# Dividing attention's output on chip, eight image rows at a time, and loading projection's input two groups ahead

## The chip, the cores and the metric

The kernel runs on one core of one Trainium2 chip. The metric is the device time of one execution in microseconds (us). The engines are named as in the profile: PE is the matrix engine (TensorE) and PEld its weight loads, DVE the vector engine, ACT the scalar engine, POOL the GpSimd engine, and SP the sync engine, which here issues every DMA. Each engine works through its own queue of instructions in order, and engines wait for one another through semaphores.

## The reference: two layers on a 48 x 48 image

The input is two images of 48 x 48 tokens with 768 channels. Two layers are applied one after the other, each added to its own input:

```
x = x + attention(groupnorm(x))     # 12 heads of 64, relative position terms, projection
x = x + spectral(groupnorm(x))      # 2-D FFT, two block-diagonal complex layers, inverse FFT
```

Only the first layer is touched by the change. Its attention, for each image and head, over S = 2304 tokens:

```
attn = (q * scale) @ k.T + rel_h[..., :, None] + rel_w[..., None, :]
attn = softmax(attn)
out  = attn @ v                     # 2304 x 64 per head
y    = out @ proj_w + proj_b        # 768 -> 768 over all heads
```

What matters here is where the softmax's division takes place. The kernel computes `exp(score - max)` without dividing, multiplies it with `v`, and scales the product by the inverse of the row's sum (the denominator) later, before projection.

## The kernel before, in words

**Stages.** For each of the two images in turn: `norm_transpose` normalises the image and lays it out with channels on partitions (`xnT`); `attention` runs all heads; `project_out` multiplies the heads' outputs with `proj_w` and adds the input; `Spectral` is the second layer. All matrix work is in 32-bit floats.

**Units of attention.** Heads are taken in six pairs (`pr`), so that two heads of 64 fill the 128 partitions. The 48 image rows are cut into six groups (`g`) of eight rows, 384 tokens; each group into three units (`x` = 0, 1, 2), 8 rows by 16 columns, 128 query tokens. The list `order` (L475) has the 108 units of an image. A unit is computed against all 2304 keys for both heads.

**What one unit needs.** `new_unit` (L340) adds the relative position terms `rhw` of rows and columns into a tile `s` of 128 x 2 x 2304: one POOL instruction a head (L344). There are four such tiles. `scores` (L354) lets PE make ten 128 x 512 pieces (the last two 128 x 256), and DVE adds each to `s` and keeps its maximum. The two heads alternate, so that DVE's second reduction is the first that needs the second head of `s`. `numerators` (L383) takes the exponential on ACT, with sums of the rows in `parts`. `squares` (L397) transposes 32 x 32 blocks on DVE, and `exchange` (L403) moves the blocks between partitions into `pT`, a quarter of them by ACT copies and the others by DMAs, six for each half of the unit. `weigh` (L417) multiplies with `v` on PE into the one bank of `ps_o`. `finish` (L434) copies that to a tile `res` of the group (ACT), reduces `parts` to a denominator (DVE, tile `dens`) and, after the group's last unit, stores `res` to the DRAM tensor `oT`.

**The order of the work.** It is written out by hand in the loop at L496. `InOrder` (L60) pins every instruction given through `pe`, `dve`, `act` and `sync` behind the one traced before it on that engine; the POOL instructions of `new_unit` are not pinned. Pass `n` runs the scores of unit `n`, the second half of the exchange of unit `n-1`, the first half of unit `n`, and the weighing of unit `n-2`; at its end `new_unit` prepares unit `n+1`. Beside the units, PE computes the queries of coming groups and the keys and values of the next head pair (`keys`, `values`, `queries`), one product a pass, so that the last pair has none of the keys and values left to make. `relative` (L289) makes the relative terms of a coming group in the pass with x = 0; they go to DRAM and come back skewed (`t<-rel`, `rhw<-t`). All matrix products but `ps_o` share seven PSUM banks in rotation (`ps_b`).

**The denominators before.** After three groups, `inverses` (L452) takes the reciprocals of 18 columns; a pass later PE transposes them (tile name `ps_i`), ACT copies them out, and three DMAs store them to the DRAM tensor `inv_d`.

**Projection before.** `Projection` (L576) lays its weights and token groups into the memory that `xnT` had. For a group of 384 tokens `parts` (L664) loads `oT` in two DMAs, loads the inverses spread over 64 partitions each in two more, and multiplies on POOL (128 x 2304). There are two buffers for tokens and one for inverses. The first steps (`late`, L533 and L560) run during the last passes of attention, and the products of the first tokens are filled in between the last units there. In `project_out` (L688) `tokens` is called one group ahead, from the loop over 18 tiles of 128 tokens, and POOL adds the bias to the rows of `x` (`rows`, L701).

Of the kernel before, what the change touches and what calls it, by code (L numbers as in the profile page):

```python
# [17 lines left out]
P = 128  # L18
HW = 48
S = HW * HW  # L20
C = 768
# [38 lines left out]
class InOrder:  # L60


    def __init__(self, tc, engine):
        self.tc, self.engine = tc, engine
# [95 lines left out]

def attention(tc, k, x_b, a, oT, inv_d, late, span, ps_b, ps_o):

# [11 lines left out]
    with ExitStack() as ctx:  # L176
# [14 lines left out]
        def bank(name):  # L191
            return ps_b.tile([P, 512], F32, tag="b", name=name)
# [12 lines left out]
        )  # L205
        bq = keep.tile([P, NP], F32, tag="bq", name="bq")
        bk = keep.tile([P, NP], F32, tag="bk", name="bk")
        rel = relp.tile([P, 2, 3, 2, RW], F32, tag="rel", name="rel")
        with ExitStack() as ctx2:
            small = ctx2.enter_context(tc.tile_pool(name="gn_s", bufs=1))  # L210
# [8 lines left out]
        pe, dve, act, sync = (  # L219
            InOrder(tc, e) for e in (nc.tensor, nc.vector, nc.scalar, nc.sync)  # L220
        )

        def project_T(w, parts):
# [116 lines left out]
        def new_unit(pr, g, x):  # L340
            qT, rhw = groups[pr, g]
            s = sp.tile([P, 2, S], F32, tag="s", name="s")
            for h in range(2):
                nc.gpsimd.tensor_tensor(  # L344
                    s[:, h, :].rearrange("p (y x) -> p y x", x=HW),
                    rhw[:, x, h, :HW][:, :, None].to_broadcast([P, HW, HW]),
                    rhw[:, x, h, HW:][:, None, :].to_broadcast([P, HW, HW]),
                    ALU.add,
                )
            return {"pr": pr, "g": g, "x": x, "qT": qT, "s": s}  # L350
# [78 lines left out]
                        skip_group_check=True,  # L429
                    )  # L430

        outs, dens = {}, {}

        def finish(un):  # L434

            pr, g, x = un["pr"], un["g"], un["x"]
            if x == 0:
                outs[pr, g] = outp.tile([P, 8, 3, 16], F32, tag="res", name="res")
                if g % 3 == 0:
                    dens[pr, g // 3] = outp.tile([P, 3, 2, 3], F32, tag="dens", name="dens")  # L440
            res = outs[pr, g]
            act.copy(res[:, :, x, :], un["o"][:, :P].rearrange("p (y d) -> p y d", d=16))
            dve.tensor_reduce(
                dens[pr, g // 3][:, x, :, g % 3], un["parts"], AX.X, ALU.add
            )
            if x == 2:
                sync.dma_start(
                    out=oT[pr * P : (pr + 1) * P, g * UQ : (g + 1) * UQ],
                    in_=res.rearrange("p y x d -> p (y x d)"),
                )  # L450

        def inverses(pr, half):  # L452


            den = dens.pop((pr, half)).rearrange("p x h g -> p (x h g)")
            inv = smallp.tile([P, 18], F32, tag="inv", name="inv", bufs=2)
            dve.reciprocal(inv, den)
            turned = outp.tile([18, P], F32, tag="turned", name="turned")

            def turn():  # L460
                tp = bank("ps_i")
                pe.transpose(tp[:18, :P], inv, k.ident)
                by_act.append(lambda: act.copy(turned, tp[:18, :P]))

            def send():
                dst = inv_d[pr, half].rearrange("h g (y x d) -> x (h g) y d", x=3, d=16)
                for x in range(3):
                    sync.dma_start(
                        out=dst[x],
                        in_=turned[6 * x : 6 * x + 6, :].rearrange("p (y d) -> p y d", d=16),  # L470
                    )

            return turn, send
# [18 lines left out]
        staged = ((0, 1), queries(0, 1))  # L492
        evict(by_act)
        recent = []
        last = turn = send = None
        for n in range(len(order) + 3):  # L496
            un = older = None
            if n < len(order):
                un = ahead
                pr, g, x = order[n]  # L500
                if g == 4 and x == 0 and pr + 1 < NP:
                    weights[0] = load_w(0, pr + 1)
                scores(un)
                recent.append(un)
            write = read = None
            if un is not None:
# [19 lines left out]
                if ready is not None:  # L526
                    key, qT = ready
                    rhw, write, read = relative(key[1], qT)
                    groups[key] = (qT, rhw)
            if turn is not None:  # L530
                turn()
                turn = None
            if n >= len(order) - 1 and recent:  # L533
                late(n - len(order) + 2)
            if n > 1 and recent:
# [3 lines left out]
            if last is not None:  # L539
                squares(last, 1)  # L540
                exchange(last, 1)
            if write is not None:
                write()
            if un is not None:
# [2 lines left out]
            evict(by_dve)  # L547
            if read is not None:
                read()
            if older is not None:  # L550
                finish(older)
            if un is not None and n + 1 < len(order):
                ahead = new_unit(*order[n + 1])
            if send is not None:
                send()
                send = None
            if older is not None and older["x"] == 2 and older["g"] % 3 == 2:
                turn, send = inverses(older["pr"], older["g"] // 3)
            if len(order) - 6 <= n <= len(order):
                late()  # L560
            last = un
# [14 lines left out]
class Projection:  # L576


    def __init__(self, tc, k, a, oT, inv_d, span, ps_b, dram):
# [3 lines left out]
        self.inv_d = inv_d  # L583
# [79 lines left out]

    def parts(self, g):  # L664

        at = [(NCC + 1) * C + i * NCC * UQ for i in range(3)]
        o_sb, inv = (
            self.whole[:, c0 : c0 + NCC * UQ].rearrange("p (cc s) -> p cc s", s=UQ)
            for c0 in (at[g % 2], at[2])
        )  # L670
        for h in range(2):
            cc = slice(h * NCC // 2, (h + 1) * NCC // 2)
            self.sync.dma_start(out=o_sb[:, cc], in_=self.oT_v[:, cc, g * UQ : (g + 1) * UQ])
            if h == 0:
                yield
        for h in range(2):
            self.sync.dma_start(
                out=inv[h * HD : (h + 1) * HD],
                in_=self.inv_d[:, g // 3, h, g % 3, :].partition_broadcast(HD),
            )  # L680
# [374 lines left out]
def block_kernel(tc, a, out):  # L1055
    nc = tc.nc
    B = a["x"].shape[0]
    with ExitStack() as ctx:
# [20 lines left out]
        for b in range(B):  # L1079
            oT = dram.tile([C, S], F32, tag=f"oT{b}", name=f"oT{b}")  # L1080
            y_d = dram.tile([YP, HW // 2, C], F32, tag=f"y_d{b}", name=f"y_d{b}")
            inv_d = dram.tile([NP, 2, 2, 3, UQ], F32, tag=f"inv_d{b}", name=f"inv_d{b}")
            ready = []

            def late(fill=0):
                if not ready:
                    ready.append(Projection(tc, k, a, oT, inv_d, span, ps_b, dram))
# [5 lines left out]
            attention(tc, k, a["x"][b], a, oT, inv_d, late, span, ps_b, ps_o)  # L1093
# [118 lines left out]
```

## Time and profile before

| what | value |
|---|---|
| runs without the profiler | median 3800.66 us of 3 (3797.74 to 3800.78) |
| the profiled execution: its time | 3804.1 us |
| its span, first to last instruction | 3802.2 us |
| mean granted clock of PE | 0.978 |
| attention of the first image, about | 70 to 1490 us |
| its projection, about | 1445 to 1640 us |
| DMA share of 16 engines, 120 to 1225 us | 0.76 |
| the same, 1225 to 1405 us (the last head pair) | 0.85 |
| POOL `s<-rhw`, 432 instructions | 1740.8 us, 4060 ns each |
| POOL idle before them | 1114.1 us |
| POOL multiply by the inverses in projection, 12 | 60.6 us |
| PE transposes of the inverses, 24 | 6.6 us |

How to read it: a row of the profile's groups names the line, the engine, the operation, what is written and read by the program's tile names, and the count; then busy time, the mean length of one, and how long the engine stood idle just before, with what ended the wait. The line of most attention instructions is L68, since `InOrder` issues them, so they are told apart by their tiles. In a timeline the first two numbers are start and length in us, "x4" is four instructions in a row, and the square bracket at the end is idle time of that engine before the row and what released it. SPq is SP's queue; its times are those of issuing a DMA, not of the transfer. In a row of windows the first numbers are the window and its length, then busy time and count for PE, PEld, DVE, ACT and POOL, then PE's granted clock, the DMA share and GB/s. A row of waits has who, for whom, the total, how many times, and the longest.

### The profile page before, as it was taken

To read this page: it belongs to the slowest core of one execution; us is meant where nothing else is said; L and a number is where in the kernel's file an instruction comes from. 1 tells how busy PE (TensorE), PEld (TensorE's weight loads), DVE (VectorE), ACT (ScalarE), POOL (GpSimd) and SP (SyncE) were. 2 spreads that over 40 slices of the span, in tenths; PEclk is the share of its full clock that TensorE was granted. 3 is DMA by queue.
4 is the path that set the end of the run, shared out by engine and by line. 5 is a ranking of instruction groups with operands and counts; after the bars stand their busy time and mean duration, and the time that the engine had idled before them with its cause. 6 is when DMAs were issued, how large, how long until landed. Compare 5 with 4: busy or idle time off the path is not lost.

```text
span 3802.2 us, 83341 instructions
## 1 busy us (share of the span) xinstructions
PE 3648.8 (96%) x31520; PEld 2592.3 (68%) x31520; DVE 2844.6 (75%) x6692; ACT 2519.5 (66%) x3692; POOL 1989.0 (52%) x598
## 2 busy tenths in 40 slices
PE   8999999999999888999989999999999999879999
PEld 6677776767777664566666767777677776645665
DVE  4788888888888983335557988889898898833445
ACT  3788888888888882133237888888888888821331
POOL 2565757575756663312125656566666666533121
PEclk9999999999999998999989999999999999889999
DMA  3677777777777887633526777777777778875334
GB/s 101 148 177 167 174 169 173 170 168 176 165 175 165 183 197 182 158 105 106 172 77 148 168 177 167 178 164 177 161 177 167 174 170 175 196 184 150 109 101 135
DMA packets 497822, 607.02 MB, mean 160 GB/s; under 512 B 180493, under 2 KB 312973, under 8 KB 497422
## 3 DMA queue, kind: packets, MB, share of 16 engines
q1 hardware_dynamic: 497422, 601.69, 67.6%
q8 instruction: 251, 4.11, 0.5%
q14 instruction: 149, 1.22, 0.1%
HBM read 131.61 MB, written 87.67 MB: 58 GB/s over the span
## 4 chain that ended last, share of the span: by engine, by line
PE 89%; DMA 4%; ACT 3%; DVE 2%; issue 1%; SPq 1%; POOL 1%; POOLq 0%; DVEq 0%; ACTq 0%
PE ps_o L68 23%; PE ps_s L68 21%; PE ps_proj L68 15%; PE ps_v L68 7%; PE acc L68 7%; PE ps L948 4%; PE ps_z L892 2%; PE ps L920 2%; PE ps_u L983 2%; PE ps L924 2%; PE ps_y L721 2%; PE ps_r L68 1%; ACT pT L68 1%; PE ps_x L1001 1%; DMA pT<-s 1%; DVE s L68 1%
## 5 line engine op out<-in xcount | busy, mean ns | idle before, releaser
L344 POOL TENSOR_TENSOR s<-rhw 128x2304 f32<-128x2304 f32 x432 | 1740.8, 4060 | 1114.1 <-DMA pT<-s 452.8
L68 DVE CUSTOM_DVE_ANT_0 s<-ps_s,s 128x512 f32<-128x512 f32 (+1 forms) x2160 | 1222.2, 633 | 359.4 <-issue 258.2
L68 ACT ACTIVATE s<-s,nm 128x1152 f32<-128x1152 f32 x864 | 1074.7, 1245 | 436.5 <-DVE nm L68 416.0
L68 DVE STREAM_TRANSPOSE s<-s 128x1152 f32<-128x1152 f32 x864 | 1111.8, 1344 | 5.5 <-ACT s L68 5.5
L68 ACT COPY pT<-s 32x1152 f32<-32x1152 f32 x864 | 993.3, 1150 | 21.5 <-PE ps_o L68 4.1
L68 PE MATMUL ps_o<-pT,v 128*64 128x128 f32 x15552 | 920.0, 278 | 49.7 <-ACT res L68 20.6
L68 PEld LDWEIGHTS ps_o<-pT,v 128*64 128x64 f32 x15552 | 868.2, 140 | 114.3 <-issue 50.7
L68 PE MATMUL ps_s<-kT,qT 64*128 64x512 f32 (+1 forms) x4320 | 908.8, 557 | 6.6 <-DVE mx L68 3.9
L68 PEld LDWEIGHTS ps_s<-kT,qT 64*128 64x128 f32 x4320 | 429.0, 186 | 436.6 <-issue 337.3
L68 PE MATMUL ps_proj<-xnT,w 128*128 128x384 f32 (+1 forms) x2016 | 596.4, 449 | 2.3 <-ACT gn_rstd L151 2.3
L68 PEld LDWEIGHTS ps_proj<-xnT,w 128*128 128x128 f32 x2016 | 360.0, 191 | 209.2 <-DVE mx L68 41.1
L68 PE MATMUL acc<-proj 128*128 128x384 f32 x864 | 288.7, 493 | 40.5 <-POOL proj L68 40.5
L742 DVE TENSOR_TENSOR x<-acc,x 32x384 f32<-32x384 f32 (+2 forms) x216 | 119.2, 553 | 276.8 <-PE acc L68 193.9
L68 PEld LDWEIGHTS ps_v<-w,xnT 128*128 128x128 f32 x2592 | 297.5, 194 | 21.2 <-DVE mx L68 21.2
L68 PE MATMUL ps_v<-w,xnT 128*128 128x128 f32 x2592 | 309.7, 279 | 0.0
L965 POOL TENSOR_TENSOR spectrum<-spectrum 128x480 f32<-128x480 f32 x80 | 96.3, 1204 | 342.0 <-DVE spectrum L964 195.8
L68 PEld LDWEIGHTS acc<-proj 128*128 128x128 f32 x864 | 166.1, 193 | 157.5 <-POOL proj L68 41.4
L728 ACT COPY y<-ps_y 112x384 f32<-112x384 f32 x96 | 46.0, 479 | 265.8 <-PE ps_y L721 264.5
L68 DVE DVE_READ_ACCUMULATOR2_ANT mx<- 128x1 f32 x2160 | 179.8, 83 | 0.0
L68 POOL TENSOR_TENSOR proj<-proj 128x2304 f32<-128x2304 f32 x12 | 60.6, 5049 | 222.4 <-DMA proj<-inv_d 185.3
L68 ACT ACTIVATION_READ_ACCUMULATOR s<-s,nm 128x1 f32 x864 | 161.1, 187 | 0.0
L928 ACT ACTIVATE spectrum<-ps,b 96x400 f32<-96x400 f32 x96 | 56.6, 590 | 146.5 <-PE ps L924 146.5
(98 smaller groups left out, 2096.5 us busy)
## 6 DMA issues: line engine op xcount, KB each, us to landing
pT<-s SPq DMA_DIRECT2D x2592, 144.0 KB
t<-rel SPq DMA_DIRECT2D x144, 189.0 KB
rhw<-t SPq DMA_DIRECT2D x144, 144.0 KB
y<-y_d SPq DMA_DIRECT2D x40, 360.0 KB
u_d<-spectrum SPq DMA_DIRECT2D x40, 360.0 KB
u<-u_d SPq DMA_DIRECT2D x48, 300.0 KB
xt<-in_x SPq DMA_DIRECT2D x12, 1152.0 KB
w<-in_qkv_w SPq DMA_DIRECT2D x36, 384.0 KB
```

The lines of the kernel that those rows point to most:

```text
L68: return lambda *args, **kw: self.tc.keep_in_program_order(op(*args, **kw))
L344: nc.gpsimd.tensor_tensor(s[:, h, :].rearrange("p (y x) -> p y x", x=HW), rhw[:, x, h, :HW][:, :, None].to_broadcast([P, HW, HW]), rhw[:, ...
L721: nc.tensor.matmul(ps[:YP, : 2 * SC], lhsT=k.fw, rhs=part[:, t0 : t0 + 2, ch], start=True, stop=True,)
L728: nc.scalar.copy(y1[:, :, ch], ps[:YP, : 2 * SC].rearrange("p (t c) -> p t c", c=SC))
L742: nc.vector.tensor_tensor(dst, acc[p : p + n, :UQ], dst, ALU.add)
L892: nc.tensor.matmul(ps[:BS, w * 96 : (w + 1) * 96], lhsT=self.y2[s, j][:, w, i * BS : (i + 1) * BS], rhs=k.fh, start=True, stop=True,)
L920: nc.tensor.matmul(ps[:BS, :400], lhsT=w1[:, wa, i, :], rhs=zf[:, 0, fs], start=True, stop=False,)
L924: nc.tensor.matmul(ps[:BS, :400], lhsT=w1[:, wb, i, :], rhs=zf[:, 1, fs], start=False, stop=True,)
L928: nc.scalar.activation(self.o1[:, ri, fs], ps[:BS, :400], AF.Gelu, bias=self.b1[:, n, ri : ri + 1])
L948: nc.tensor.matmul(ps[64 * r : 64 * r + 64, w * BS : (w + 1) * BS], lhsT=self.o1[:, ri, f0 : f0 + 64], rhs=w2[:, (0, 2, 1, 0)[2 * r + ri], ...
L965: nc.gpsimd.tensor_tensor(val, val, clip, ALU.subtract)
L983: nc.tensor.matmul(ps[: 2 * HW, :480], lhsT=k.ih, rhs=d2[:, c0 : c0 + 480], start=True, stop=True)
```

## The change

Attention now divides each group itself. In the pass after a group's last unit had its scores, `inverses` reduces the unit's sums, takes the reciprocal of a 128 x 32 tile `den` (six columns of it in use, all others one), transposes it in 32 x 32 blocks on DVE and stores it to a small DRAM tile. The function that it returns, `fetch`, is called a pass later, between the two halves of the exchange; it reads the inverses back in two DMAs, each spread over 64 partitions in runs of 96 numbers. When the group's last `res` copy is done, the next pass begins with `divide`, two POOL multiplies of 128 x 192; `store` sends `res` to `oT` in that pass, ahead of the first half of its exchange. The POOL instructions of `new_unit` are now pinned in program order too. The loop has one pass more. The PE transposes, their ACT copies and the three stores for every three groups are gone.

Projection loads `oT` alone, in two DMAs a group, into three buffers, and no longer multiplies. `tokens(2)` comes in the last step of attention, and from then on groups come two ahead, after the rows' loads.

```diff
-                nc.gpsimd.tensor_tensor(
+                pool_e.tensor_tensor(
                     s[:, h, :].rearrange("p (y x) -> p y x", x=HW),
...
+        def inverses(un):
+            key, x = (un["pr"], un["g"]), un["x"]
+            dve.tensor_reduce(
+                den[:, :6].rearrange("p (h x) -> p h x", x=3)[:, :, x], un["parts"], AX.X, ALU.add
+            )
+            if x < 2:
+                return None
+            turned = outp.tile([P, 32], F32, tag="turned", name="turned")
+            dve.reciprocal(turned, den)
+            dve.transpose(turned, turned)
+            inv_d = dp.tile([P * 32], F32, tag="inv_d", name="inv_d")
+            sync.dma_start(out=inv_d.rearrange("(p i) -> p i", i=32), in_=turned)
+
+            def fetch():
+                over[key] = inv = smallp.tile([P, 4, 3, 32], F32, tag="inv", name="inv", bufs=1)
+                for h in range(2):
+                    sync.dma_start(
+                        out=inv[h * HD : (h + 1) * HD].rearrange("p b x i -> p b (x i)"),
+                        in_=bass.AP(
+                            inv_d.tensor, inv_d.offset + 96 * h, [[0, HD], [1024, 4], [1, 96]]
+                        ),
+                    )
+            return fetch
+
+        def divide(key):
+            res = outs[key].rearrange("p (b y) x d -> p b y x d", y=2)
+            inv = over.pop(key).rearrange("p b x (y d) -> p b y x d", y=2)
+            for y in range(2):
+                pool_e.tensor_tensor(res[:, :, y], res[:, :, y], inv[:, :, y], ALU.mult)
...
-        for n in range(len(order) + 3):
+        for n in range(len(order) + 4):
             un = older = None
+            if whole is not None:
+                divide(whole)
...
-            if turn is not None:
-                turn()
-                turn = None
...
                 exchange(last, 1)
+            if whole is not None:
+                store(whole)
+                whole = None
+            if fetch is not None:
+                fetch()
+                fetch = None
             if write is not None:
                 write()
...
+            if last is not None:
+                fetch = inverses(last)
             if older is not None:
                 finish(older)
+                if older["x"] == 2:
+                    whole = older["pr"], older["g"]
...
-            if send is not None:
-                send()
-                send = None
-            if older is not None and older["x"] == 2 and older["g"] % 3 == 2:
-                turn, send = inverses(older["pr"], older["g"] // 3)
...
-            lambda: next(parts),
             lambda: list(parts),
             lambda: self.tokens(1),
+            lambda: self.tokens(2),
...
+        c0 = (NCC + 1) * C + g % 3 * NCC * UQ
+        self.o[g] = self.whole[:, c0 : c0 + NCC * UQ].rearrange("p (cc s) -> p cc s", s=UQ)
         for h in range(2):
             cc = slice(h * NCC // 2, (h + 1) * NCC // 2)
-            self.sync.dma_start(out=o_sb[:, cc], in_=self.oT_v[:, cc, g * UQ : (g + 1) * UQ])
-            if h == 0:
-                yield
-        for h in range(2):
-            self.sync.dma_start(
-                out=inv[h * HD : (h + 1) * HD],
-                in_=self.inv_d[:, g // 3, h, g % 3, :].partition_broadcast(HD),
-            )
-            if h == 0:
-                yield
-        self.pool.tensor_tensor(o_sb, o_sb, inv, ALU.mult)
-        self.o[g] = o_sb
-        yield
+            self.sync.dma_start(out=self.o[g][:, cc], in_=self.oT_v[:, cc, g * UQ : (g + 1) * UQ])
+            yield
...
         if t % 3 == 0 and 0 < t < NT - 3:
-            pr.tokens(t // 3 + 1)
             rows(t // 3 + 1)
+            if t < NT - 6:
+                pr.tokens(t // 3 + 2)
```

More of the change, by code (lines that the diff above doesn't have):

```diff
@@ L159, in norm_transpose, with attention @@
             )
-def attention(tc, k, x_b, a, oT, inv_d, late, span, ps_b, ps_o):
+def attention(tc, k, x_b, a, oT, late, span, ps_b, ps_o):
     nc = tc.nc
@@ L207, in attention @@
         bk = keep.tile([P, NP], F32, tag="bk", name="bk")
+        den = keep.tile([P, 32], F32, tag="den", name="den")
+        nc.gpsimd.memset(den, 1.0)
         rel = relp.tile([P, 2, 3, 2, RW], F32, tag="rel", name="rel")
@@ L218, in attention @@
         nc.vector.tensor_scalar(bk, bk, HD**-0.5, None, ALU.mult)
-        pe, dve, act, sync = (
-            InOrder(tc, e) for e in (nc.tensor, nc.vector, nc.scalar, nc.sync)
+        pe, dve, act, pool_e, sync = (
+            InOrder(tc, e) for e in (nc.tensor, nc.vector, nc.scalar, nc.gpsimd, nc.sync)
         )
@@ L430, in weigh @@
                     )
-        outs, dens = {}, {}
+        outs, over = {}, {}
+        def inverses(un):
[20 more added lines that the diff above has]
+            return fetch
@@ L434, in finish @@
         def finish(un):
-            pr, g, x = un["pr"], un["g"], un["x"]
+            key, x = (un["pr"], un["g"]), un["x"]
             if x == 0:
[L438 to L444, printed above, removed]
-            )
@@ L446, in finish @@
[L446 to L449, printed above, removed]
-                )
[L452 to L473, printed above, removed]
+                outs[key] = outp.tile([P, 8, 3, 16], F32, tag="res", name="res")
@@ new lines, in finish, with store @@
+            act.copy(outs[key][:, :, x, :], un["o"][:, :P].rearrange("p (y d) -> p y d", d=16))
+        def divide(key):
[3 more added lines that the diff above has]
+                pool_e.tensor_tensor(res[:, :, y], res[:, :, y], inv[:, :, y], ALU.mult)
+        def store(key):
+            pr, g = key
+            sync.dma_start(
+                out=oT[pr * P : (pr + 1) * P, g * UQ : (g + 1) * UQ],
+                in_=outs.pop(key).rearrange("p y x d -> p (y x d)"),
+            )
@@ L494, in attention @@
         recent = []
-        last = turn = send = None
-        for n in range(len(order) + 3):
+        whole = last = fetch = None
+        for n in range(len(order) + 4):
             un = older = None
+            if whole is not None:
+                divide(whole)
             if n < len(order):
@@ L576, with __init__ @@
 class Projection:
-    def __init__(self, tc, k, a, oT, inv_d, span, ps_b, dram):
+    def __init__(self, tc, k, a, oT, span, ps_b, dram):
         self.nc = nc = tc.nc
@@ L582, in __init__ @@
         self.oT_v = oT.rearrange("(cc p) s -> p cc s", p=P)
-        self.inv_d = inv_d
         self.whole = span.tile([P, NCC * S], F32, tag="span", name="proj")
@@ L664, in parts @@
     def parts(self, g):
[L666 to L670, printed above, removed]
+        c0 = (NCC + 1) * C + g % 3 * NCC * UQ
+        self.o[g] = self.whole[:, c0 : c0 + NCC * UQ].rearrange("p (cc s) -> p cc s", s=UQ)
         for h in range(2):
             cc = slice(h * NCC // 2, (h + 1) * NCC // 2)
-            self.sync.dma_start(out=o_sb[:, cc], in_=self.oT_v[:, cc, g * UQ : (g + 1) * UQ])
-            if h == 0:
-                yield
-        for h in range(2):
-            self.sync.dma_start(
-                out=inv[h * HD : (h + 1) * HD],
-                in_=self.inv_d[:, g // 3, h, g % 3, :].partition_broadcast(HD),
-            )
-            if h == 0:
-                yield
-        self.pool.tensor_tensor(o_sb, o_sb, inv, ALU.mult)
-        self.o[g] = o_sb
-        yield
+            self.sync.dma_start(out=self.o[g][:, cc], in_=self.oT_v[:, cc, g * UQ : (g + 1) * UQ])
+            yield
 def project_out(tc, k, x_b, pr, pools, y_d, x2, constants):
@@ L1081, in block_kernel @@
             y_d = dram.tile([YP, HW // 2, C], F32, tag=f"y_d{b}", name=f"y_d{b}")
-            inv_d = dram.tile([NP, 2, 2, 3, UQ], F32, tag=f"inv_d{b}", name=f"inv_d{b}")
             ready = []
@@ L1086, in late @@
                 if not ready:
-                    ready.append(Projection(tc, k, a, oT, inv_d, span, ps_b, dram))
+                    ready.append(Projection(tc, k, a, oT, span, ps_b, dram))
                 if fill:
@@ L1091, in late @@
                     ready[0].step()
-            attention(tc, k, a["x"][b], a, oT, inv_d, late, span, ps_b, ps_o)
+            attention(tc, k, a["x"][b], a, oT, late, span, ps_b, ps_o)
             with ExitStack() as ctx2:
```

## The prediction

> **What bounds the kernel now.** I read the page first, then who waited for whom on TensorE, then stages by window, then the timeline at the two places where the change acts.
>
> ```profile
> PE 3648.8 (96%) x31520; PEld 2592.3 (68%) x31520; DVE 2844.6 (75%) x6692; ACT 2519.5 (66%) x3692; POOL 1989.0 (52%) x598
> ```
>
> ```profile
> PE acc L68 <- POOL proj L68: 40.5, 2, 23.0
> ```
>
> ```profile
> 120.00:1225.00 1105.00, 1105.00 (x10317) 805.42 (x10315) 968.55 (x2304) 916.66 (x1261) 705.27 (x176) 1.00 0.76 170
> ```
>
> PE (TensorE) is the bound; its largest wait is for POOL (GpSimd) in projection, 40.5 us in two pieces, one an image. In the window that covers nearly all of head pairs 0 to 4 of the first image PE has no idle time at all (1105.00 of 1105.00). A PE delay there is paid in full.
>
> The two pieces, from PE's timeline at the end of attention:
>
> ```profile
> 1439.93 4.14 PE L68 MATMUL ps_pb<-proj,bv 128*128 128x384 f32 x12
> 1461.56 6.90 PE L68 MATMUL acc<-proj 128*128 128x384 f32 x12 [17.48 <-POOL proj L68]
> ...
> 3357.02 10.24 PE L68 MATMUL acc<-proj 128*128 128x384 f32 x24 [23.02 <-POOL proj L68]
> ```
>
> and what POOL waited for in the first:
>
> ```profile
> 1456.47 5.03 POOL L68 TENSOR_TENSOR proj<-proj 128x2304 f32<-128x2304 f32 x1 [37.99 <-DMA proj<-inv_d]
> ```
>
> The second half of the inverses is issued on SP at 1448.4, behind twelve pT transfers, lands at 1456.3, POOL multiplies until 1461.5, then PE starts.
>
> **Gains.** (1) The inverse loads and the 5 us multiply in front of the first product go. In the first image PE was free at 1444.1; the second oT half was issued at 1435.2. Next late is unit 106's pT, landed at 1448.4, just after the product. So the 17.5 us go, and 2.8 more because the product after the wait took 6.90 for 4.1 (clock 0.84 in this stretch). I keep 20. In the second image oT's last half was issued at 3330.7, just ahead of an inverse load landing at 3340.5; halving that queue puts oT near 3337, 3 us after PE is free: 23.0 + 2.1 - 3 = 22. (2) Twenty-four PE transposes go (row `ps_i` below, 273 ns of duration; in the chain of waits each takes 0.21): 5. Sum 47. Later projection groups already cost PE nothing: PE is busy 148.85 of 150 us in 1490 to 1640. The other removed work (12 POOL multiplies after the first, 24 ACT copies, 72 small stores) was beside PE and is worth nothing.
>
> **Costs.** Each group of eight rows now puts two small multiplies on POOL, in program order ahead of the bias sums `s` of a coming group. Today POOL runs ahead and needs only the rel-pos reads; afterwards it must also have the finished group's last `res` copy and the fetched inverses. One group in the steady stretch:
>
> ```profile
> 606.93 16.11 POOL L344 TENSOR_TENSOR s<-rhw 128x2304 f32<-128x2304 f32 x4 [12.12 <-DMA rhw<-t]
> ...
> 612.79 0.27 ACT L68 COPY res<-ps_o 128x128 f32<-128x128 f32 x1
> ...
> 601.82 1.26 SPq L68 DMA_DIRECT2D rhw<-t  x2
> 605.05 8.11 SPq L68 DMA_DIRECT2D pT<-s  x12
> ...
> 621.04 0.69 DVE L68 CUSTOM_DVE_ANT_0 s<-ps_s,s 128x512 f32<-128x512 f32 x1 [1.25 <-issue]
> ...
> 621.66 0.69 DVE L68 CUSTOM_DVE_ANT_0 s<-ps_s,s 128x512 f32<-128x512 f32 x1
> ```
>
> Read it so: POOL fills the x=0 unit of group G+2 from 606.93 to 615.0; DVE needs its second head at 621.66. The multiply for group G now stands before it. `res` of G's last unit is done at 613.06; with POOL's semaphore wait, 613.4. The fetch is issued after the sixth of the twelve pT issues (the seventh starts at 609.0). Its landing: the rhw reads take a median 5.5 us from first issue to POOL's start; the fetch has 512 packets for their 1,536, and 1,024 fewer at some 25 ns (the trace's mean for such packets) on 16 engines save 1.6: 3.9, so 612.8. `res` decides here; elsewhere, often the fetch. A multiply, from the groups by form (mean ns of one behind the busy time):
>
> ```profile
> L68 POOL TENSOR_TENSOR proj<-proj 128x2304 f32<-128x2304 f32 x12 | 60.6, 5049 | 222.4 <-DMA proj<-inv_d 185.3
> ...
> L68 POOL TENSOR_TENSOR x<-x,proj 96x768 f32<-96x768 f32 x48 | 85.2, 1808 | 1.2 <-PE ps_o L68 1.1
> ...
> L68 PE MATMUL ps_i<-ident,inv 128*18 128x128 f32 x24 | 6.6, 273 | 0.0
> ```
>
> The first two rows give 2.11 ns an element and 187 ns a call: 192 elements cost 0.59, two 1.2 (bounds 0.9 and 1.6, if short strided runs run faster or slower). Then 613.4 + 1.2 + 8.1 = 622.7: DVE's second head is 1.0 us late. Reading the same times for all groups with G+2 in pairs 0 to 4 (56, both images) gives late by 0.3 to 1.8, mean 1.0. PE feels it through the seven PSUM banks: the product after the scores needs the bank that DVE's fourth reduction frees (here 623.57), and today starts 0.28 us after that, at 623.85. Of this some 0.2 is slack, so PE stops 0.8: 56 x 0.8 = 45. PE cannot win it back, and SP, ACT and DVE behind it follow PE, so it repeats in every group. In the last pair PE has no next projections; pT packets end 3 us after issue instead of 1.5, so the fetch is later: late by 1.6 on average over 12 groups; DVE idles only some 14 us in 180 there (166.14 busy), so 1.4 each passes on: 17.
>
> DVE gets, per group, a wider reciprocal and a 128x32 transpose, some 0.4 us by the 128x18 reciprocal (0.27) and the 128x1152 transpose (1.34); in pairs 0 to 4 DVE waits 1.25 us or more before each unit's first reduction, so nothing; in the last pair 12 x 0.4, of which I count 2. Were that cover gone it would be 29 in all. The denominators' reduction only moves within its pass. SP gets three issues of 0.6 a group in place of one: store, write and fetch stand before pT transfers needed two passes later, and SP idles 2 us (603.1 to 605.05) and 3.5 us (613.8 to 617.3) before these pT batches, so nothing; without that slack the issues would be 72 x 1.2 us of SP time. The multiply's result is stored one pass later, long before its reader. Sum of costs: 45 + 17 + 2 = 64.
>
> **Two rules against the rows.** The Trainium skill, "DMA: Bandwidth & Descriptors", section "Anatomy of one DMA", puts a transfer (fitted on software-made descriptors) at about 2.0 us plus bytes over 436 GB/s. As an estimate the fetch would reach POOL about 3 us after its issue, `res` alone would decide, late would fall to some 0.75, costs to 45: no change. I take the rhw row's 3.9, measured behind the same pT queue. "GPSIMD Engine Reference", section "Engine selection", gives elementwise products to VectorE. There, two of 192 elements would take about 0.7 by the 384-element `x<-acc,x` row (0.55), inside DVE's idle time, POOL would never be late, and only the 47 gained would remain. The change takes POOL: its queue, not its speed, is what costs.
>
> **Rivals.**
> - *The lateness is absorbed* (faster): the multiply starts or runs 0.3 us sooner, or PE has more bank slack. From a mean lateness of about 0.8 down the 47 wins; at 0.4, costs are about 20: 3774. For it: half of the lateness is an extrapolated 1.2 us. Against: not one of the 68 groups reads on time. 22%.
> - *The fetch is held by its own write*: `inv_d`'s write goes out behind the rhw reads, about 603, and lands perhaps at 608; the fetch could go at 608.9. If the write takes 1 to 2 us longer, SP holds the fetch and the pT transfers behind it, and POOL is later by as much: 68 more per us, about 3890. For it: a margin of 1 us; against: SP waited for its `t<-rel` writes only four times, 5.3 us in all. 16%.
> - *The wait at the first product is not removed* but passes to oT's load or to the weights: the gain halves, 3840. 6%.
>
> **How the numbers follow.** 3804.1 for the profiled execution (span 3802.2 and 1.9 around it), minus 47, plus 64: 3821. The median of the runs is 3.4 lower: 3818. This case has 56% and its own range 3793 to 3850 (late by 0.75 to 1.4); within it 44% slower, 10% same, 2% faster. Within 0.2% (7.6 us) of before is what a measurement here can't tell from no change. With the rivals: faster 0.22, same 0.12, slower 0.66. The range 3778 to 3866 takes in most of the first rival and leaves out the worse half of the second.
>
> **What would show it.** Right: in the page POOL's idle time before `s<-rhw` is ended by ACT `res`, or by the inverse fetch through the multiply; DVE's reductions wait for POOL `s` in most groups, about 1 us each; PE idle before `ps_proj` or `ps_v` some 45 us, ended by DVE; `acc` waits for POOL gone; two multiplies of 0.6. Wrong: PE still at 1105 of 1105 in pairs 0 to 4, or multiplies far from 0.6, or SP waiting for DMA `inv_d<-turned`.

## The result, and the profile after

The changed kernel takes 3877.89 us (median of 4 runs, 3875.04 to 3890.09), the kernel before in the same series 3799.2 (4 runs, 3792.48 to 3800.78): ratio 1.0216 [1.0201, 1.0231]. Slower, as predicted, but by 79 us where 17 were forecast. The profiled execution took 3879.6 us, with a span of 3877.8 against 3802.2: 75.6 to explain.

Engine totals (the page) and the window that before was 1105.00 of 1105.00 for PE:

```profile
PE 3720.3 (96%) x31496; PEld 2605.6 (67%) x31496; DVE 2885.5 (74%) x6812; ACT 2515.7 (65%) x3668; POOL 2006.8 (52%) x732
```

```profile
120.00:1225.00 1105.00, 1089.37 (x9879) 775.38 (x9876) 948.29 (x2268) 880.69 (x1205) 699.41 (x223) 1.00 0.75 169
```

PE now has holes in this window, and 9879 products fall into it where 10317 did. The waits:

```profile
POOL res L68 <- DMA inv<-inv_d: 990.3, 69, 26.4
...
DVE s L68 <- POOL s L68: 169.6, 84, 22.8
...
PE ps_s L68 <- DVE mx L68: 61.0, 59, 2.8
```

and, in the kernel before, DVE's row for POOL's bias sums:

```profile
DVE s L68 <- POOL s L344: 54.6, 21, 23.0
```

PE's row for POOL in projection is gone. In its place POOL waits for the fetched inverses ahead of 69 of its 72 pairs of multiplies, DVE for POOL's bias sums 84 times (21 before), PE for DVE 59 times. PE's timeline at both images' first projection products shows the gain that was hoped for (the first row is the work in front of the first image's; the last two rows are the second image's):

```profile
1498.76 4.14 PE L68 MATMUL ps_pb<-proj,bv 128*128 128x384 f32 x12
1502.73 4.03 PE L68 MATMUL acc<-proj 128*128 128x384 f32 x12
...
3434.47 2.20 PE L68 MATMUL acc<-proj 128*128 128x384 f32 x6
3438.82 6.07 PE L68 MATMUL acc<-proj 128*128 128x384 f32 x18 [2.15 <-DMA proj<-oT]
```

In the first image no wait is left. In the second one of 2.15 us is left after six products, and the oT load ends it.

To place the 75.6 us I cut both executions at the same instructions: DVE's `nm` reductions (each follows the last piece of a unit's scores) of units 6, 90 and 107, the last `res` copy, and the last product of projection. The two images stand before and after the plus sign; the last column is the prediction's sum.

| stretch | before | after | moved | predicted |
|---|---|---|---|---|
| pairs 0 to 4 (unit 6 to 90) | 1056.1 + 1056.0 | 1099.4 + 1106.5 | +93.9 | +40 (45, less 5 for PE transposes) |
| last pair (unit 90 to 107) | 204.5 + 208.1 | 217.8 + 217.1 | +22.2 | +19 (17 and 2) |
| unit 107 to the last `res` | 53.9 + 55.3 | 33.6 + 33.0 | -42.6 | -42 |
| last `res` to the end of projection | 153.5 + 149.7 | 153.5 + 149.6 | 0 | 0 |
| everything else | | | +2 | 0 |

One term is wrong: pairs 0 to 4. One group there, somewhat later than most, in the order POOL, SP, ACT, DVE, PE (each from that engine's timeline):

```profile
634.28 1.14 POOL L68 TENSOR_TENSOR res<-res,inv 128x192 f32<-128x192 f32 x2 [15.96 <-DMA inv<-inv_d]
635.38 24.15 POOL L68 TENSOR_TENSOR s<-rhw 128x2304 f32<-128x2304 f32 x6
...
629.12 1.30 SPq L68 DMA_DIRECT2D inv<-inv_d  x2
...
632.40 0.27 ACT L68 COPY res<-ps_o 128x128 f32<-128x128 f32 x1
...
643.49 0.69 DVE L68 CUSTOM_DVE_ANT_0 s<-ps_s,s 128x512 f32<-128x512 f32 x1 [2.13 <-POOL s L68]
...
639.41 3.70 PE L68 MATMUL ps_s<-kT,qT 64*128 64x512 f32 x16
644.25 1.31 PE L68 MATMUL ps_s<-kT,qT 64*128 64x256 f32 x4 [1.13 <-DVE mx L68]
```

`res` is ready at 632.67. The fetch is issued at 629.12, but POOL's multiplies start only at 634.28, 5.16 us after it. They end at 635.4; two bias sums of 4.06 follow, up to 643.46, and at 643.49 DVE makes the reduction that had waited 2.13. PE then stands 1.13 us as the row shows, and its four small products take 1.31 where a twenty-product batch without a wait takes 4.14 in all, which is 0.46 for these four by their columns: 0.85 more of waiting lies inside the row. PE loses 1.98 (1.13 and 0.85) of DVE's 2.13.

Over the 56 groups whose delay falls into the first row of the table, the time from the fetch's issue to the multiply has a mean of 4.88 us (3.9 was taken), the multiply begins 1.47 after `res`, the pair of multiplies takes 1.14 (1.2 was taken), and DVE waits 1.65 (1.0 was taken for late).

### The profile page after: what moved, and what is told of

Its sections match the earlier page's. It is cut to its first block, busy times and chain, and to the rows that moved or that the text cites. A ratio compares the mean times of both kernels' runs of the same rounds, so it can differ in the third digit from the quotient of the medians.

```text
span 3877.8 us, 83832 instructions
## 1 busy us (share of the span) xinstructions
PE 3720.3 (96%) x31496; PEld 2605.6 (67%) x31496; DVE 2885.5 (74%) x6812; ACT 2515.7 (65%) x3668; POOL 2006.8 (52%) x732
## 3 DMA queue, kind: packets, MB, share of 16 engines
q14 instruction: 153, 1.25, 0.1%
## 4 chain that ended last, share of the span: by engine, by line
PE 50%; DVE 17%; POOL 13%; DMA 8%; SPq 8%; issue 3%; ACT 1%; POOLq 0%; DVEq 0%; ACTq 0%
DVE s L68 15%; POOL s L68 13%; PE ps_o L68 10%; SPq L68 8%; PE acc L68 7%; PE ps_s L68 7%; PE ps_v L68 6%; DMA pT<-s 6%; PE ps_proj L68 5%; PE ps L946 4%; PE ps L918 2%; PE ps_u L981 2%; PE ps_z L890 2%; PE ps L922 2%; PE ps_y L718 1%
## 5 line engine op out<-in xcount | busy, mean ns | idle before, releaser
L68 PE MATMUL ps_s<-kT,qT 64*128 64x512 f32 (+1 forms) x4320 | 972.6, 562 | 64.2 <-DVE mx L68 61.0
L68 POOL TENSOR_TENSOR res<-res,inv 128x192 f32<-128x192 f32 x144 | 82.5, 594 | 1069.0 <-DMA inv<-inv_d 990.3
L926 ACT ACTIVATE spectrum<-ps,b 96x400 f32<-96x400 f32 x96 | 56.6, 590 | 145.8 <-PE ps L922 145.8
```

What stands on the lines that cost most here:

```text
L68: return lambda *args, **kw: self.tc.keep_in_program_order(op(*args, **kw))
L926: nc.scalar.activation(self.o1[:, ri, fs], ps[:BS, :400], AF.Gelu, bias=self.b1[:, n, ri : ri + 1])
```

## The experiments

The theory from the two traces: the gain is as predicted, and the loss is POOL's lateness, of which the fetch's landing, not `res` and not the multiplies, is the greater part. Rival: something else in the change slows pairs 0 to 4 (the multiplies themselves, the pinning, the extra SP issues, the write).

**The multiplies behind the bias sums.** POOL's order alone is changed; the store of `res` goes out a pass later.

```diff
-            if whole is not None:
-                divide(whole)
...
             if un is not None and n + 1 < len(order):
                 ahead = new_unit(*order[n + 1])
+            if whole is not None:
+                divide(whole)
+                done, whole = whole, None
```

> The change with one move: the two multiplies of a finished group stand behind, not ahead of, the bias sums of the next group's first unit on POOL (and the store one pass later). Theory (place in POOL's queue): in pairs 0 to 4 the 94 us lost there go, in the last pair most of the 22, while the 43 won at the first product and the transposes' 5 stay: 3755 us, 3745 to 3770; DVE hardly ever waits for POOL's sums. Rival (the added DMA issues and small packets delay the pT transfers, or DVE's extra work): the multiplies' place is indifferent, 3850 to 3880.

3762.38 us, ratio to before 0.9905 [0.9887, 0.9923]. Pairs 0 to 4 take 1056.4 + 1055.0, what they took before. The multiply's row in the groups:

```profile
L68 POOL TENSOR_TENSOR res<-res,inv 128x192 f32<-128x192 f32 x144 | 82.9, 597 | 107.7 <-ACT res L68 64.2 <-DMA inv<-inv_d 43.5
```

As many multiplies, equally long, and 43.5 us of waiting for the fetch in place of 990.3. The same work with the same SP issues costs nothing once the sums that DVE waits for stand ahead of it. That rules out the multiplies, the pinning, the SP issues and the write as costs of their own in pairs 0 to 4.

**No wait for the inverses.** The multiplies stay in front but take a constant tile of ones; the fetch is still issued. Attention's output stays undivided here.

```diff
-                pool_e.tensor_tensor(res[:, :, y], res[:, :, y], inv[:, :, y], ALU.mult)
+                pool_e.tensor_tensor(
+                    res[:, :, y],
+                    res[:, :, y],
+                    one[:, None, :, :].to_broadcast([P, 4, 3, 16]),
+                    ALU.mult,
+                )
```

> The change with its multiplies taken by a constant one in place of the fetched inverses, which are still computed, stored and fetched, but not used: the output is left undivided. The multiplies keep their place in POOL's queue and wait for the res copy alone. In the changed kernel the multiply starts 1.5 us after res on average in pairs 0 to 4 and 2.1 in the last pair. Theory: those 1.5 go from a loss of 1.8 a group, 56 x 1.5 = 84 and about 19 in the last pair: 3775 us, 3760 to 3800. If the multiplies' own length and the res copy set the delay: 3850 or more. Rival (DMA or DVE load): 3878.

3780.80 us, ratio 0.9952 [0.9937, 0.9967].

```profile
L68 POOL TENSOR_TENSOR res<-res,ones 128x192 f32<-128x192 f32 x144 | 82.3, 592 | 970.1 <-ACT res L68 864.8 <-issue 69.0 <-DMA inv<-inv_d 25.1
```

The multiply now starts 0.08 us after `res`, DVE waits 0.28 on average, pairs 0 to 4 take 1061.1 + 1060.8. So `res` and two multiplies in front of the sums cost some 10 us in pairs 0 to 4; the wait for the fetch costs the other 84 of the 94, the clock (below) included.

**The same bytes in long runs.** The inverses are written so that the 384 of a head lie together: the two fetches have 128 packets of 1,536 bytes in place of 512 of 384. The tile's layout follows; the multiplies still take 592 ns.

```diff
-            sync.dma_start(out=inv_d.rearrange("(p i) -> p i", i=32), in_=turned)
+            sync.dma_start(
+                out=bass.AP(inv_d.tensor, inv_d.offset, [[32, 4], [128, 32], [1, 32]]),
+                in_=turned,
+            )
...
-                            inv_d.tensor, inv_d.offset + 96 * h, [[0, HD], [1024, 4], [1, 96]]
+                            inv_d.tensor, inv_d.offset + 384 * h, [[0, HD], [1, 384]]
```

> The change with the inverses laid out in DRAM so that a head's 384 are contiguous: the fetch reads one run of 1536 bytes for each partition in place of four of 384 (128 packets for 512); the write has as many runs as before. In the changed kernel the fetch's packets span 2.6 us, from 1.4 to 4.0 after its issue, though 512 packets of 22 ns on 16 engines fill only 0.7. If the number of runs makes that span, the last packet comes at about 2.8, the landing 1.2 us sooner, 56 x 1.2 and some 14 in the last pair: 3797 us, 3785 to 3815. If it is a fixed latency of a read through two issues: 3870 to 3880.

3808.54 us (13 runs), ratio 1.0021 [1.0012, 1.003].

```profile
L68 POOL TENSOR_TENSOR res<-res,inv 128x192 f32<-128x192 f32 x144 | 82.3, 592 | 994.5 <-DMA inv<-inv_d 582.6 <-ACT res L68 373.2 <-DMA pT<-s 25.1
```

From issue to multiply it is now 3.8 us on average, close to the 3.9 that the prediction took. `res` and the fetch share the releases, as the prediction had read from the trace of before. DVE waits 0.68, pairs 0 to 4 take 30.3 more than before and the last pair 14. With about the landing that was assumed, the kernel's time is within 10 us of the 3818 that was predicted, so this run isolates the term that failed. It is below 3818 because another term was too high (POOL's start after `res`, next section): pairs 0 to 4 lose 30 where 40 were predicted.

**The fetch sooner.** It is issued ahead of the second half of the exchange, six pT transfers earlier.

```diff
             evict(by_act)
+            if fetch is not None:
+                fetch()
+                fetch = None
             if last is not None:
                 squares(last, 1)
                 exchange(last, 1)
...
-            if fetch is not None:
-                fetch()
-                fetch = None
             if write is not None:
                 write()
```

> The change with the fetch issued one batch of six pT transfers earlier in the same pass. It would be issued some 4.4 us sooner, about 3.8 us after its own write was issued. Theory: res becomes the last thing that the multiply waits for, as with no wait for inverses: 3775 us, up to 3800 as the pT issues come 1.3 us later. Rival (the write's landing holds the fetch, and SP with it): SP waits for inv_d<-turned in every group, the fetch gains only part of the 4.4, 3800 to 3870.

3861.41 us, ratio 1.0159 [1.0133, 1.0186]: the rival's range, not the theory's. SP's waits for the inverses' write, here and (second row) in the changed kernel as it is:

```profile
SPq L68 <- DMA inv_d<-turned: 223.6, 72, 4.6
...
SPq L68 <- DMA inv_d<-turned: 5.3, 6, 2.9
```

PE's waits for pT, here and (second row) before:

```profile
PE ps_o L68 <- DMA pT<-s: 86.3, 53, 7.0
...
PE ps_o L68 <- DMA pT<-s: 18.9, 8, 4.6
```

POOL is hardly late here: DVE's second reduction, the one that waited 1.65 us after the change, waits 0.04 on average. But SP, in order, stands in each of the 72 groups for the inverses' write to land, 3.1 us on average (223.6 / 72), and the pT transfers queued behind go out late. In pairs 0 to 4, which take 61.8 us more than before, PE now waits 56.6 us ahead of `ps_o` products (0.2 before). The wait did not go, it changed its queue.

**The multiplies on DVE**, with the order of the first experiment.

```diff
-                pool_e.tensor_tensor(res[:, :, y], res[:, :, y], inv[:, :, y], ALU.mult)
+                dve.tensor_tensor(res[:, :, y], res[:, :, y], inv[:, :, y], ALU.mult)
```

> The change with the multiplies on DVE instead of POOL, at the end of the same pass, when the inverses have long landed. Theory (place in POOL's queue): POOL is never late, DVE takes about 0.7 us a group into its waits of 1.25 us before each unit; only the last pair, where DVE has little idle time, may give back 12 x 0.7 = 8: 3765 us, 3755 to 3775, like the kernel with the sums first. Rival (DVE has no room): 36 groups x 2 x 0.7 = 50 more, 3810.

4006.08 us, ratio 1.055 [1.0527, 1.0573]: far outside both. The operation's own record (min, median and max in ns), then one pair on DVE's timeline and the sums on POOL's:

```profile
L68 DVE TENSOR_TENSOR res<-res,inv x144: 342/1854/4209, 166.9 to 3586.1; 128x192 f32<-128x192 f32 x144
```

```profile
575.12 4.40 DVE L68 TENSOR_TENSOR res<-res,inv 128x192 f32<-128x192 f32 x2
...
566.94 12.09 POOL L68 TENSOR_TENSOR s<-rhw 128x2304 f32<-128x2304 f32 x3
```

The first multiply starts just after POOL began the third sum (about 575.0) and ends about 0.2 us after that sum does, at 579.03 (566.94 + 12.09); the second, with POOL idle, takes 0.35. So throughout: 38 multiplies that met no POOL instruction take 0.346, at most 0.36; the 106 that met one take a median 2.84, up to 4.21, and 105 of them end 0.2 to 0.3 us after that sum. Pairs 0 to 4 grow by 200 us, of which some 69 are PE's clock (see the run with a second multiply).

**Projection's groups one ahead**, the change otherwise whole (one late step fewer goes with it).

```diff
-            lambda: self.tokens(2),
...
-            if t < NT - 6:
-                pr.tokens(t // 3 + 2)
+            pr.tokens(t // 3 + 1)
```

> The change with projection's groups coming one ahead, as before. Theory: the gain at the first product is that of the loads and the multiply taken away, and a group's load has a whole group's products (some 25 us) to land: 3878 us, no difference from the changed kernel (within 8). Rival (two ahead is what removes the wait): PE waits for proj<-oT before the second or third group, 5 to 10 us an image, 3890 to 3900.

3889.21 us, ratio 1.0234 [1.0213, 1.0255]. That is 11 us above the change, just more than the 8 allowed for, but the interval overlaps the change's. The stretches at the end of attention and in projection agree with the change's (68.6 against 66.6 us, and 303 in both). So the rival's waits in projection aren't there; whether two ahead is worth a few us elsewhere can't be told from these runs.

**Before, with POOL's sums pinned in program order** (`pool_e` in place of `nc.gpsimd` in `new_unit`).

> The kernel before with POOL's bias sums pinned in program order, and nothing else. Theory: they run in this order anyway and no multiply stands ahead of them: 3799 us, no difference. Rival (the pinning itself makes POOL late): a part of the 94 us lost in pairs 0 to 4 shows up, 3820 or more.

3801.1 us (12 runs), ratio 1.0004 [0.9993, 1.0014]: pinning costs nothing that these runs can show.

**Before, without the inverses in projection.** Neither their loads nor the multiply remain there; the division is left out.

```diff
-            self.sync.dma_start(
-                out=inv[h * HD : (h + 1) * HD],
-                in_=self.inv_d[:, g // 3, h, g % 3, :].partition_broadcast(HD),
-            )
...
-        self.pool.tensor_tensor(o_sb, o_sb, inv, ALU.mult)
```

> The kernel before, whose projection neither loads the inverses nor multiplies by them: the division is left out, though the inverses are still made and stored, and tokens still come one ahead. Theory: this is the whole gain at the end of attention, 42 us, and nothing else changes: 3757 us, 3750 to 3765; PE's wait for POOL's proj gone. Rival (the wait passes to the next late thing, oT or pT): less than half of it, 3780 or more.

3757.35 us, ratio 0.9893 [0.9875, 0.9911]. The end of attention takes 33.6 + 34.7 us, as after the change: nearly all of the -42.6 by itself.

**A second multiply.** After each multiply by the inverses comes one by ones, which leaves the values as they are: about 1.2 us more on POOL for each group.

```diff
                 pool_e.tensor_tensor(res[:, :, y], res[:, :, y], inv[:, :, y], ALU.mult)
+                pool_e.tensor_tensor(
+                    res[:, :, y],
+                    res[:, :, y],
+                    one[:, None, :, :].to_broadcast([P, 4, 3, 16]),
+                    ALU.mult,
+                )
```

> The change with each of its two multiplies followed by a second one of the same size by a constant one on POOL, ahead of the bias sums. Theory (every delay at this place in POOL's queue is paid by PE, without slack): 2 x 0.57 = 1.14 us more for each of 56 groups in pairs 0 to 4 and about as much for 12 in the last pair, 78 us more than 3878: 3955 us, 3940 to 3965. Rival (part of the delay is absorbed downstream): 3900 to 3930.

4056.09 us, ratio 1.0673 [1.0655, 1.069]: 178 more than the change, where 78 were expected. (The profiled execution was the fastest of the five, 147.5 us above the change's; what follows is read from it.) The multiplies are no longer than before (595 ns), so the price of a late us was about twice what was expected. In the first image's group at 615 us, PE's timeline, and then windows of 1 us there (PE busy, PE's granted clock, DMA share, GB/s):

```profile
620.71 3.70 PE L68 MATMUL ps_s<-kT,qT 64*128 64x512 f32 x16
626.89 1.83 PE L68 MATMUL ps_s<-kT,qT 64*128 64x256 f32 x4 [2.48 <-DVE mx L68]
628.65 6.95 PE L68 MATMUL ps_proj<-xnT,w 128*128 128x384 f32 x12
```

```profile
625.00:626.00 1.00, 0.00 (x0) 1.00 0.91 233
626.00:627.00 1.00, 0.11 (x1) 1.00 0.99 230
627.00:628.00 1.00, 1.00 (x3) 0.76 0.93 226
628.00:629.00 1.00, 1.00 (x3) 0.50 0.37 81
...
633.00:634.00 1.00, 1.00 (x3) 0.50 0.00 0
634.00:635.00 1.00, 1.00 (x4) 0.83 0.00 0
```

After a hole of 2.48 us the granted clock falls to 0.50 for 7 us, and twelve products that take 4.14 elsewhere take 6.95. Adding up one minus the clock over pairs 0 to 4 gives the time lost to it: 0 before, 9.1 us after the change, 70.4 here. Of the 126.5 us by which pairs 0 to 4 grew against the change, 61.3 are the clock; the other 65.2 are 1.16 for each of 56 groups. That is about the POOL time added, and about what DVE's second reduction waits longer (2.82 against 1.65). So the term that this run was to measure is confirmed at about 1 to 1 in pairs 0 to 4, and a second one came with it. (The sum takes PE as busy while its clock is low, as it is in the window shown.) The last pair grew by 15.7 us, but by 15.1 in the same sum of the clock: the 14 expected there from the multiplies' own time aren't seen, and why is open.

**Sums first, long runs, and the fetch behind the first half of the next exchange**: what the runs pointed to.

```diff
             if un is not None and n + 1 < len(order):
                 ahead = new_unit(*order[n + 1])
+            if whole is not None:
+                divide(whole)
+                done, whole = whole, None
...
                 exchange(un, 0)
+            if fetch is not None:
+                fetch()
+                fetch = None
```

> The kernel with the sums first, its inverses in long runs, and the fetch issued behind the second batch of pT transfers of its pass instead of ahead of it. The multiply there has some 2 us to spare after the landing, and long runs land 1.2 us sooner. Theory (the fetch has slack now, pT transfers should not stand behind it): no worse than 3762 us, at best the 3757 of the kernel without any inverses in projection; 3755 to 3764. Rival (the multiply becomes late again, now for the sums of the group's second unit, which have about 2 us to spare): 3775 or more.

3756.54 us, ratio 0.9882 [0.9867, 0.9897], the fastest version; its interval overlaps that of sums-first alone (0.9905), so the two further steps aren't shown to gain. In the window of pairs 0 to 4 PE is whole again:

```profile
120.00:1225.00 1105.00, 1105.00 (x10309) 804.79 (x10306) 984.37 (x2357) 917.12 (x1254) 735.73 (x234) 1.00 0.78 175
```

## Why the prediction was right in sign and wrong in size

- **Gain at projection's first product, -42.** Right: -20.3 and -22.3. The oT load is late next in the second image, as said, by 2.15 us after six products.
- **PE transposes, -5.** Too high: in the fastest version, where PE has no hole in the window shown, pairs 0 to 4 take 2.1 less than before.
- **The failed step: the fetch's landing, "the fetch has 512 packets for their 1,536 ... 3.9".** It took the rhw reads' 5.5 us and took off packets at their mean time spread over 16 engines. Measured from issue to multiply: 4.88 in pairs 0 to 4, 5.01 in the last pair. The first packet comes 1.4 us after the issue and the last ends at 4.0 (medians), though 512 packets at their mean 25 ns over 16 engines fill only 0.8. So a mean packet time over 16 engines does not give a landing; with 128 packets for the same bytes the last ends at 3.0. "`res` decides here; elsewhere, often the fetch" turned with it: the fetch decided in 69 of 72 groups, and late was 1.65 by DVE's wait, not 1.0. The rest of that sum holds: read from the trace of before for the same groups, it gives 0.99 with 3.9 and 1.84 with 4.88.
- **A term of that sum that was too high**, and hid a part of the error: "with POOL's semaphore wait, 613.4". POOL starts 0.08 after `res` when it waits for that alone, not 0.34 as there, and late is then 0.28, where the prediction had 0.75.
- **"Of this some 0.2 is slack".** About right, if anything too much: (93.9 + 2.1 - 9.1) / 56 = 1.55 of 1.65 reaches PE; 1.98 of 2.13 in the group shown.
- **A term missing among the costs: PE's clock.** 9.1 us in pairs 0 to 4. In the last pair the same sum is 34.2, against 27.3 before: up to 6.9 of its 22.2. That is an upper bound, since PE is not always busy there, and it differs between executions (39.3 in the run with projection's groups one ahead).
- **The last pair, +19.** Near at +22.2, but partly by chance: DVE's second reduction waits 2.5 us there, not the 1.6 taken for late, so less of it passed on than the prediction held, and a part of the loss is the clock.
- **The pairs 0 to 4 together.** They lost 93.9 where 40 were predicted. Of the 54 between, 42 are the lateness (56 groups at 1.55 in place of 0.8), 9 the clock and 3 the transposes.
- **Multiplies at 0.59.** Right, 594 ns. DVE's extra work was 0.35 + 0.21 = 0.56 for the 0.4 taken; the 2 us for it are a part of the last pair's 19 and weren't measured apart.
- **Where PE would stand.** Predicted before `ps_proj` or `ps_v`; it is at the last four score products, which need the same late bank, and a part of the wait is inside their length.
- **The rival "held by its own write"** named 3890, near the result, but that is chance: SP waits 5.3 us for that write in all. The run that moved the fetch ahead shows what that rival costs when it is real.
- **The rules weighed against the rows.** By "Engine selection" of "GPSIMD Engine Reference" the prediction put the product on VectorE at 0.7 a group, with the whole 47 gained. That product measures 2.14 us for one multiply on average, and the kernel 244 us more than with the multiply on POOL in the same order (4006.08 against 3762.38). The other rule, from "DMA: Bandwidth & Descriptors", section "Anatomy of one DMA", gave an estimate of 3 us for what took 4.88; the row, too low at 3.9, was the nearer.

Open: what spreads the last packet to 4.0 us after the issue (the pT transfers of the same queue run on both sides of it), which holes bring PE's clock down, and what two groups ahead is worth.

## What to carry to other kernels

Work put in front of an in-order engine's queue inherits the latest of its inputs, and everything queued behind inherits that; find the first instruction behind it that someone waits for, and put the work after that one: in pairs 0 to 4 the same two multiplies cost 94 us ahead of the bias sums and next to nothing behind them. Take a small transfer's landing from one with a like number and length of packets, and carry its error through the sum: one us of landing was worth about 60 us in pairs 0 to 4 here (63.6 us for 1.06, the clock included). Where the bounding engine is PE, a stall of a us or more may be charged again through its clock.

## What was not expected of the hardware

- **PE's clock can drop after short holes.** With the doubled multiplies, 31 of 56 holes of 1 to 3 us in PE's rows (pairs 0 to 4) were followed within 5 us by a granted clock of 0.50, for 3.4 or 6.8 us; after the change 5 of 16 holes of 1 us or more, each for 3.4 us, and none of 16 between 0.5 and 1. Length alone does not decide: with the doubled multiplies holes of 1.25 us were followed by the low clock and one of 2.78 was not, and with the fetch ahead of the exchange only 2 of 27 holes over 1 us were. The Trainium skill, "TensorE: Matmul & The Clock Gate", section "HAM oscillation — how this bites in real kernels", warns of idle gaps beyond about 3.4 us; by that rule nothing would have been charged in the changed kernel, whose longest hole there is 2.01 us, some 2.9 with the 0.85 that can lie inside the next products. The bound itself isn't measured.
- **A DVE product of two SBUF tiles does not run beside POOL.** 0.346 us alone, a median 2.84 and up to 4.21 beside a POOL sum of 4.06, ending just after it. "GPSIMD Engine Reference", section "Specifications", mentions contention for instructions with two SBUF inputs; here it lasts until POOL's instruction is over. DVE's score reductions, which take one input from PSUM, keep their 0.69 beside the same sums.
- **The same bytes land sooner in fewer, longer packets.** 4.88 us to the multiply with 512 packets, 3.8 with 128 four times as long (where the multiply waited for `res` in 27 of 72 groups, so the landing itself is a little sooner). Number and length changed together here.
- **A small write to DRAM holds a reader close behind it.** With the fetch moved ahead, SP stood 3.1 us for the write (223.6 us over 72 waits), and issued the fetch 3.9 us after it had issued the write (mean of pairs 0 to 4).
